# Joining loads in pairs and groups, and quantising two pieces at a time, in a fused two-layer Mamba, BitNet, attention and expert kernel

## The chip, the cores and the metric

The kernel runs on one core of a Trainium2 chip. The metric is device time in microseconds (us) of one launch. The core has five engines that work side by side, each through its own instructions in program order: TensorE (PE), VectorE (DVE), ScalarE (ACT), GpSimd (POOL) and SyncE (SP). In this kernel SP does nothing but issue DMAs, all of them, so every load, store and DMA transpose stands in one queue, and one that waits for its source or for a free buffer holds back all behind it.

## The reference

The input `x` has 4 batches of 512 rows of 512 features; `ctx` has 4 batches of 512 rows of 256. Two layers follow each other, each a mixer and a feed-forward part, both added to `x` through a tanh gate:

```
x = x + tanh(g_xattn[0]) * mamba(ctx_1024, layernorm(x))
x = x + tanh(g_ffn[0])   * bitnet_glu(layernorm(x))
x = x + tanh(g_xattn[1]) * cross_attention(layernorm(x), ctx_1024)
x = x + tanh(g_ffn[1])   * experts(layernorm(x))
```

- Mamba: 512 channels with 16 states each. For state n, step l: `state = state * exp(delta*A) + (delta*u) * B[n, l]` and `y += state * C[n, l]`. B and C are rows of 512 numbers, the same for all channels.
- BitNet GLU: three linear maps with activations rounded to 8-bit integers and ternary weights; `out(silu(gate(x)) * val(x))`, with 2048 inner values per row, gate and value biases, and a second rounding of the inner values with one scale per row.
- Cross attention: 16 heads of 128, queries and keys normalised, softmax over 512 keys, output projection `Wo`.
- Experts: four gated maps, each for a fixed quarter of the rows.

## The kernel before

Activations lie with 128 rows on the 128 partitions, so each batch is four blocks (`T = 4`). Products that need more than half precision use three matmuls on high and low f16 parts (`mm3`). A tile framework records the whole program, gives out buffers from tagged pools, and fixes the order of instructions on each engine with its own timing model; the recorded order sets the priorities. So a changed buffer or instruction also moves others.

**Stages, with their place in the profiled execution.** Weights are staged and the scan of batch 0 runs from about 55 to 180 us. The GLU of batch 0 and the staging of attention weights follow, to about 340 us. Then attention runs, 64 heads (4 batches, 16 heads), two heads ahead in the queries (a loop over `i`). Into the attention of batches 0, 1 and 2 the generator `layer0(b)` weaves scan and GLU of the next batch. Into the attention of batch 3 the experts of the first three batches are filled (`early_experts`); those of batch 3 end the kernel (`last_experts`).

**The scan (`scan`).** For batch 0 the four channel blocks are done together (`G = 4`), later two and two. For each state n the rows B[n] and C[n] are read from the DRAM scratch `bd`, each by its own DMA, and laid on all 128 partitions (`bc`, `cc`: lines 612 and 614). For each channel block ACT computes `dA = exp(delta*A)`, POOL computes `h = du * bc` (line 186, through `pool_mult`), DVE runs the recurrence (line 625, or 628 where POOL multiplies afterwards), and DVE (line 626) or POOL multiplies by `cc`. PE then transposes `h` and sums it in PSUM (line 593). `h` has six buffers under the tag `v`, shared with others.

**The GLU (`bitnet`).** `hidden(t)` makes the 2048 inner values of block t in four pieces `g` of 128x512. In batches 1 to 3 the tile of each piece is first filled with the gate bias by a DMA (line 709); DVE adds it to the scaled product (line 711). `project(t)` finds the row scale over all four pieces, and for each piece ACT scales and rounds (line 747) and DVE clamps to bf16 (line 748); pairs of pieces are transposed by DMA (line 750) and multiplied by the output weights. `hidden(t + 1)` is recorded before `project(t)`.

**The tag `g`.** `bc`, `cc`, the GLU's pieces and the experts' inner values (`it`, four for each expert, which all feed the down products `ped`) share six buffers of 2 KB a partition: `MIDS = {"g": 6, ...}`.

**Attention.** After each group of four heads `project(hg, os)` multiplies by the group's part of `Wo`: four loads of 256 KB into the tag `wo` with `WO = 4` buffers (line 977), and 4 x 12 matmuls `pwo`. For each half head SP also issues a transpose of the weights (`pT`, line 950), and for each block of keys two of `kT` (line 847). A softmax uses exp; the Ln of delta, the tanh of the GLU and the Silu of the experts need other ACT tables, so where these alternate in ACT's order, the compiler puts table loads.

Of the kernel before, what the change touches and what calls it, by code (L numbers as in the profile page):

```python
# [29 lines left out]
F32 = mybir.dt.float32  # L30
F16 = mybir.dt.float16
# [3 lines left out]
AF = mybir.ActivationFunctionType  # L35
# [5 lines left out]
P = 128  # L41
B = 4
L = 512
# [20 lines left out]
DVE_OF_8 = (0, 1, 2, 4, 5, 6)  # L64


MIDS = {"g": 6, "v": 6, "t": 4, "q": 2, "n": 1, "x": 1, "y": 2}
FILL0 = 4
RATE_S = 0.5
RATE_B = 0.8  # L70
# [40 lines left out]
def flamingo_kernel(  # L111
# [460 lines left out]
    def scan(b, of_8=DVE_OF_8, G=2, y_tile=lambda name: psum(pss, name), between=lambda n, ins: None):  # L572
        delta, du, ud_d, bd = fronts[b]
        sz_d = dram.tile([P, T, L], F32, tag="szd", name=f"szd{b}", bufs=2)

        def silu_z(t):

            xt = x_sb[b]
            w = normed(xt[:, t, :], row_stats(xt[:, t, :], f"z{b}{t}", 0.5), f"z{b}{t}")
            th = midt([P, L], F32, f"zth{b}{t}", "t")  # L580
            nc.scalar.activation(th, w, AF.Tanh)
            nc.vector.scalar_tensor_tensor(w, th, 1.0, w, ALU.add, ALU.mult)
            return w

        for t0 in range(0, T, G):
            gs = T // G
            ys = [y_tile(f"py{b}{t0}{i}").rearrange("p (g t e) -> p g t e", g=gs, t=G) for i in range(G)]

            def add(src, t, first, last):
                for g in range(T):
                    nc.tensor.matmul(  # L593
                        ys[g // gs][:, g % gs, t, :], src[:, g::T], ident, is_transpose=True,
                        start=first and t == 0 and g % gs == 0, stop=last, skip_group_check=True,
                    )

            uds, szs = [], []
            for t in range(G):
                uds.append(midt([P, L], F32, f"udr{b}{t0}{t}", "t"))  # L600
                nc.sync.dma_start(uds[t], ud_d[:, t0 + t, :])
            for n in range(DS):
                if n == 4 and x_sb[b] is None:
                    while b >= 2 and estats[b - 2] is None:
                        yield
                    load_x(b)
                if n == SZR and t0 > 0:
                    for t in range(t0, t0 + G):
                        szs.append(midt([P, L], F32, f"szr{b}{t}", "v"))
                        nc.sync.dma_start(szs[-1], sz_d[:, t, :])  # L610
                bc = midt([P, L], F32, f"bc{b}{t0}_{n}", "g")
                nc.sync.dma_start(bc, bd[n, :].partition_broadcast(P))
                cc = midt([P, L], F32, f"cc{b}{t0}_{n}", "g")
                nc.sync.dma_start(cc, bd[DS + n, :].partition_broadcast(P))
                for t in range(G):
                    nm = f"{b}{t0}{t}_{n}"
                    dA = psum(pss, f"dA{nm}")
                    last = nc.scalar.activation(  # L618
                        dA, delta[t0 + t], AF.Exp, scale=A[:, t0 + t, n : n + 1]
                    )  # L620
                    h = midt([P, L], F32, f"h{nm}", "v")
                    pool_mult(h, du[t0 + t], bc)

                    if (G * n + t) % 8 in of_8:
                        nc.vector.tensor_tensor_scan(dA, dA, h, 0.0, ALU.mult, ALU.add)  # L625
                        nc.vector.tensor_tensor(h, dA, cc, ALU.mult)  # L626
                    else:
                        nc.vector.tensor_tensor_scan(h, dA, h, 0.0, ALU.mult, ALU.add)
                        pool_mult(h, h, cc)
                    add(h, t, n == 0, n == DS - 1)  # L630
                    if n == 2:
                        add(uds[t], t, False, False)
                between(n, last.ins)
                yield

            xt = x_sb[b]
            if t0 == 0:
                szs = [silu_z(t) for t in range(T)]
                for t in range(G, T):
                    nc.sync.dma_start(sz_d[:, t, :], szs[t])  # L640
            for g in range(T):
                if g % gs == 0:
                    acc = midt([P, gs, G, P], F32, f"acc{b}{t0}{g}", "t")
                    nc.scalar.copy(acc, ys[g // gs])
                ps = transposed(pss, szs[:G], f"psz{b}{t0}{g}", g)
                a = acc[:, g % gs]
                nc.vector.tensor_tensor(a, a, ps, ALU.mult)
                xv = xt[:, g, :].rearrange("q (p e) -> q p e", e=T)[:, :, t0 : t0 + G]
                nc.vector.scalar_tensor_tensor(
                    xv, a.rearrange("q e p -> q p e"), tg[:, 0:1], xv, ALU.mult, ALU.add  # L650
                )
                yield
# [20 lines left out]
    def bitnet(b, w_tile=bigt, ps_tile=lambda name: psum(pss, name), biases=None, then=lambda t: None, g_tile=lambda name: psum(pss, name)):  # L673
# [23 lines left out]
        def hidden(t, xqT, sgv):  # L697

            nm = f"{b}{t}"
            hs = []  # L700
            mx = sm(4, "hmx", f"hmx{nm}")
            for n in range(4):
                cols = slice(n * 512, (n + 1) * 512)
                pg = g_tile(f"pg{nm}{n}")
                for k in range(T):
                    nc.tensor.matmul(pg, xqT[:, k, :], wg[:, k, cols], start=k == 0, stop=k == T - 1)
                g = midt([P, 512], F32, f"g{nm}{n}", "g")
                if biases is None:
                    nc.sync.dma_start(g, gate_b[cols].partition_broadcast(P))
                gb = g if biases is None else biases[0][:, cols]  # L710
                nc.vector.scalar_tensor_tensor(g, pg, sgv[:, 0:1], gb, ALU.mult, ALU.add)

                th = pg
                nc.scalar.activation(th, g, AF.Tanh, scale=0.5)
                pv = ps_tile(f"pv{nm}{n}")
                for k in range(T):
                    nc.tensor.matmul(pv, xqT[:, k, :], wv[:, k, cols], start=k == 0, stop=k == T - 1)
                v = midt([P, 512], F32, f"gv{nm}{n}", "v")
                if biases is None:
                    nc.sync.dma_start(v, val_b[cols].partition_broadcast(P))  # L720
                vb = v if biases is None else biases[1][:, cols]
                if (b, n) in GVP:
                    v2 = midt([P, 512], F32, f"gv2{nm}{n}", "t")
                    nc.scalar.activation(v2, pv, AF.Copy, scale=sgv[:, 1:2])
                    nc.gpsimd.tensor_tensor(v, v2, vb, ALU.add)
                else:
                    nc.vector.scalar_tensor_tensor(v, pv, sgv[:, 1:2], vb, ALU.mult, ALU.add)  # L727
                pool_mult(g, g, v)
                nc.vector.scalar_tensor_tensor(g, th, 1.0, g, ALU.add, ALU.mult)
                nc.vector.tensor_reduce(mx[:, n : n + 1], g, AX.X, ALU.max, apply_absolute_value=True)  # L730
                hs.append(g)
                yield

            return hs, mx

        def project(t, hs, mx):
# [2 lines left out]
            po = ps_tile(f"po{nm}")  # L739
            for i in range(2):  # L740
                hq = midt([P, 2, 512], BF16, f"hq{nm}{i}", "q" if b else "t")
                for j in range(2):
                    h = hs[2 * i + j]
                    if (b, 2 * i + j) in HQD:
                        nc.vector.tensor_scalar(h, h, up2, MAGIC, ALU.mult, ALU.add)
                    else:
                        nc.scalar.activation(h, h, AF.Identity, bias=magic, scale=up2)
                    nc.vector.tensor_scalar(hq[:, j], h, MAGIC, 127.0, ALU.subtract, ALU.min)
                hqT = midt([P, 8, P], BF16, f"hqT{nm}{i}", "q")
                nc.sync.dma_start_transpose(hqT, hq.rearrange("p j c -> p (j c)"))  # L750
                for k in range(8):
                    nc.tensor.matmul(po, hqT[:, k, :], wo[:, 8 * i + k, :], start=i + k == 0, stop=i == 1 and k == 7)
                yield
# [28 lines left out]
    def attention(b):  # L782
# [186 lines left out]
        def project(hg, os):  # L969
# [1 line left out]
            fo = sm(1, "fo", f"fo{nm}")  # L971
            nc.vector.tensor_scalar(fo, Sc[b][:, 0:1], Sv[hg][:, 0:1], 1.0 / QS, ALU.mult, ALU.mult)
            nc.vector.tensor_scalar(fo, fo, So[hg][:, 0:1], tg[:, 1:2], ALU.mult, ALU.mult)
            wos = []
            for h in range(HG):
                wo = at.tile([P, 2, 512], F16, tag="wo", name=f"wo{nm}{h}", bufs=WO)
                nc.sync.dma_start(wo.rearrange("p s c -> p (s c)"), wo_d[hg][:, h * 1024 : (h + 1) * 1024])
                wos.append(wo)
            for t in (T - 1, *range(T - 1)):
                rows = slice(t * P, (t + 1) * P)  # L980
                ps = ap(f"pwo{nm}{t}")
# [391 lines left out]
```

## Time and profile before

| | |
|---|---|
| time, median of 3 runs (lowest to highest) | 2031.38 us (2028.97 to 2038.59) |
| the profiled execution's own time | 2046.98 us |
| its span, first to last instruction | 2044.4 us |
| mean granted TensorE clock | 0.867 |
| busy: PE, DVE, ACT, POOL | 1613.0, 1576.5, 1321.8, 1000.7 us |
| DMA queue | 367.37 MB, 70.8% of 16 engines' span |
| issues on SP: `bc`, `cc` | 112 and 112, 256 KB each |
| issues on SP: gate bias `g`, `wo` | 48 and 64, 256 KB each |

The profile page gives, for one execution, the busy time of each engine, the same in 40 slices, and groups of equal instructions with their busy time, mean duration in ns, and the idle time of their engine just before them with what ended it. Other views of the same trace list instructions in order of time, waits by who waited for whom, the issues of SP with the time to landing, and busy time in chosen stretches. The profiled execution took 15.6 us longer than the median of the runs.

### The profile page before, as it was taken

How to read it: one execution, taken by the hardware profiler on the slowest of the kernel's cores; microseconds unless marked ns; L12 is line 12 of the kernel's file. 1: busy time of each engine (PE TensorE's matmuls, PEld its weight loads, DVE VectorE, ACT ScalarE, POOL GpSimd, SP SyncE). 2: the span in 40 equal slices, each digit the busy share in tenths (PEclk: the TensorE clock that was granted, in tenths of full speed). 3: DMA queues.
4: the chain of work that ended last, by engine and by line, in shares of the span. 5: the costliest groups of instructions: out<-in, count | busy, mean ns of one | idle time of the engine just before them, and what ended most of it. 6: DMA issues, size and time to landing. Idle time of an engine off the chain costs nothing. (4 is left out here: it accounts for less than half of the span.)

```text
span 2044.4 us, 27093 instructions
## 1 busy us (share of the span) xinstructions
PE 1613.0 (79%) x8238; PEld 903.5 (44%) x8238; DVE 1576.5 (77%) x2857; ACT 1321.8 (65%) x3118; POOL 1000.7 (49%) x926
## 2 busy tenths in 40 slices
PE   4465867666899877778988878778898879788888
PEld 1343322444544344454444444454444445445456
DVE  5898885999989788998987876999874455554554
ACT  5796566764758595665568663756477485757663
POOL 1884342875746378574436582765354240313211
PEclk8555987767889988898998988999999889898889
DMA  7554567788797877776658777787765686866754
GB/s 271 176 184 163 154 168 228 186 230 254 187 274 163 211 183 173 207 173 178 122 147 211 183 166 189 160 202 182 167 129 117 141 200 166 201 165 150 186 131 142
DMA packets 528242, 369.09 MB, mean 181 GB/s; under 512 B 425248, under 2 KB 427424, under 8 KB 521696
## 3 DMA queue, kind: packets, MB, share of 16 engines
q1 hardware_dynamic: 528096, 367.37, 70.8%
q8 instruction: 64, 1.05, 0.2%
q14 instruction: 82, 0.67, 0.1%
HBM read 220.22 MB, written 44.30 MB: 129 GB/s over the span
## 5 line engine op out<-in xcount | busy, mean ns | idle before, releaser
L186 POOL TENSOR_TENSOR h<-u,bc 128x512 f32<-128x512 f32 x256 | 337.6, 1339 | 83.9 <-PE py L593 49.1
L593 PE MATMUL py<-ident,h 128*128 128x128 f32 x1024 | 197.2, 337 | 134.3 <-DVE h L626 111.0
L618 ACT ACTIVATE dA<-delta,A 128x512 f32<-128x512 f32 x256 | 172.1, 685 | 136.0 <-DVE h L626 109.5
L625 DVE TENSOR_TENSOR_SCAN dA<-dA,h 128x512 f32<-128x512 f32 x200 | 240.7, 1217 | 20.3 <-POOL h L186 15.6
L252 PE MATMUL pav<-pT,v 128*128 128x256 f16 x1536 | 213.3, 294 | 49.2 <-DMA pT<-hl 36.2
L252 PE MATMUL ps<-kT,qT 128*128 128x512 f16 x768 | 215.9, 403 | 44.4 <-ACT pr L927 36.6
L252 PE MATMUL pq<-axnT,wq 128*128 128x512 f16 x768 | 211.6, 432 | 40.8 <-DMA axnT<-xsa 11.6
L593 PEld LDWEIGHTS py<-ident,h 128*128 128x128 f32 x1024 | 162.9, 212 | 179.2 <-DVE h L626 134.5
L948 DVE SCALAR_TENSOR_TENSOR hl<-pr,den,hl 128x512 f16<-128x512 f32 x214 | 195.2, 931 | 32.3 <-ACT hl L945 16.2
L907 DVE TENSOR_REDUCE nmx<-ps 128x1 f32<-128x512 f32 x256 | 172.6, 679 | 58.1 <-PE ps L252 57.5
L927 ACT ACTIVATE pr<-ps,nmx,rqs 128x512 f32<-128x512 f32 x256 | 197.6, 774 | 19.2 <-DVE hl L948 15.0
L252 PEld LDWEIGHTS <-v 128*128 128x128 f16 x1536 | 160.8, 106 | 110.1 <-issue 46.4
L252 PE MATMUL pwo<-wo,oT 128*128 128x512 f16 x768 | 184.7, 391 | 6.6 <-DVE oT L244 2.8
L947 POOL TENSOR_SCALAR hl<-pr,den 128x512 f16<-128x512 f32 x86 | 60.9, 708 | 213.8 <-issue 110.0
L252 PEld LDWEIGHTS <-wq 128*128 128x128 f16 x768 | 83.9, 110 | 153.8 <-issue 73.5
L252 PEld LDWEIGHTS <-cT 128*128 128x128 f16 x768 | 81.4, 107 | 137.5 <-issue 67.7
L186 POOL TENSOR_TENSOR g<-g,gv 128x512 f32<-128x512 f32 x64 | 83.7, 1309 | 110.3 <-DVE gv L727 55.5
L252 PEld LDWEIGHTS <-qT 128*128 128x128 f16 x768 | 78.5, 103 | 131.6 <-issue 64.4
L183 POOL TENSOR_TENSOR rqs<-ssq,mhalf 128x4 f32<-128x4 f32 x64 | 69.6, 1088 | 136.7 <-ACT ssq L896 133.7
L626 DVE TENSOR_TENSOR h<-dA,cc 128x512 f32<-128x512 f32 x200 | 133.5, 677 | 2.6
L252 PE MATMUL pk<-wk,cT 128*128 128x512 f16 x384 | 111.3, 437 | 23.8 <-DMA wk<-dwk 15.2
L945 ACT ACTIVATE hl<-pr,den 128x512 f16<-128x512 f32 x128 | 92.1, 719 | 56.1 <-DVE den L934 48.6
(373 smaller groups left out, 3512.6 us busy)
## 6 DMA issues: line engine op xcount, KB each, us to landing
bc<-bd SPq DMA_DIRECT2D x112, 256.0 KB, 4.3
cc<-bd SPq DMA_DIRECT2D x112, 256.0 KB, 4.2
wq<-dwq SPq DMA_DIRECT2D x64, 256.0 KB, 4.1
wo<-dwo SPq DMA_DIRECT2D x64, 256.0 KB, 4.4
w<-w3d SPq DMA_DIRECT2D x12, 1024.0 KB, 7.7
g<-in_gate_b SPq DMA_DIRECT2D x48, 256.0 KB, 4.3
gv<-in_val_b SPq DMA_DIRECT2D x48, 256.0 KB, 4.2
de<-hle SPq DMA_DIRECT2D x9, 1024.0 KB, 5.8
```

The lines of the kernel that those rows point to most:

```text
L183: nc.gpsimd.tensor_tensor(res, arg, mhalf[:, : arg.shape[1]], ALU.pow)
L186: nc.gpsimd.tensor_tensor(out, a, b, ALU.mult)
L252: nc.tensor.matmul(ps, l, r, start=first and i == 0, stop=last and i == n - 1)
L593: nc.tensor.matmul(ys[g // gs][:, g % gs, t, :], src[:, g::T], ident, is_transpose=True, start=first and t == 0 and g % gs == 0, stop=last ...
L618: last = nc.scalar.activation(dA, delta[t0 + t], AF.Exp, scale=A[:, t0 + t, n : n + 1])
L625: nc.vector.tensor_tensor_scan(dA, dA, h, 0.0, ALU.mult, ALU.add)
L626: nc.vector.tensor_tensor(h, dA, cc, ALU.mult)
L907: nc.vector.tensor_reduce(nmx[:, c : c + 1], ps, AX.X, ALU.max, negate=True)
L927: mark[0] = nc.scalar.activation(pr, scs[c], AF.Exp, bias=nmx[:, one], scale=rqs[:, one], accum_out=den[:, c - c0 : c - c0 + 1],).ins
L945: nc.scalar.activation(hl[:, c, 0], prs[c], AF.Copy, scale=den[:, one])
L947: nc.gpsimd.tensor_scalar(hl[:, c, 0], prs[c], den[:, one], 1.0, ALU.mult, ALU.mult)
L948: nc.vector.scalar_tensor_tensor(hl[:, c, 1], prs[c], den[:, one], hl[:, c, 0], ALU.mult, ALU.subtract)
```

## The change

Four edits. (1) B[n] and C[n] of a state come by one DMA of 512 KB into one tile `bcc` of two rows, and `bc`, `cc` are its halves; the tag `g` has three buffers of 4 KB in place of six of 2 KB. (2) The GLU's pieces lie in pairs in one tile `g2`; in batches 1 to 3 one DMA brings the gate bias of a pair. (3) A pair is rounded by one ACT and clamped by one DVE instruction of 128x1024. (4) A head group's output weights come by one DMA of 1 MB into one buffer `wo`. The experts' `it` tiles are as they were, but now share three buffers.

```diff
-MIDS = {"g": 6, "v": 6, "t": 4, "q": 2, "n": 1, "x": 1, "y": 2}
+MIDS = {"g": 3, "v": 6, "t": 4, "q": 2, "n": 1, "x": 1, "y": 2}
...
-                bc = midt([P, L], F32, f"bc{b}{t0}_{n}", "g")
-                nc.sync.dma_start(bc, bd[n, :].partition_broadcast(P))
-                cc = midt([P, L], F32, f"cc{b}{t0}_{n}", "g")
-                nc.sync.dma_start(cc, bd[DS + n, :].partition_broadcast(P))
+                bcc = midt([P, 2, L], F32, f"bcc{b}{t0}_{n}", "g")
+                nc.sync.dma_start(bcc, bd.rearrange("(s n) l -> n s l", s=2)[n].partition_broadcast(P))
+                bc, cc = bcc[:, 0], bcc[:, 1]
...
-                g = midt([P, 512], F32, f"g{nm}{n}", "g")
-                if biases is None:
-                    nc.sync.dma_start(g, gate_b[cols].partition_broadcast(P))
+                if n % 2 == 0:
+                    g2 = midt([P, 2, 512], F32, f"g{nm}{n}", "g")
+                    if biases is None:
+                        nc.sync.dma_start(
+                            g2.rearrange("p a c -> p (a c)"),
+                            gate_b[n * 512 : (n + 2) * 512].partition_broadcast(P),
+                        )
+                    hs.append(g2)
+                g = g2[:, n % 2]
...
-                for j in range(2):
-                    h = hs[2 * i + j]
-                    if (b, 2 * i + j) in HQD:
-                        nc.vector.tensor_scalar(h, h, up2, MAGIC, ALU.mult, ALU.add)
-                    else:
-                        nc.scalar.activation(h, h, AF.Identity, bias=magic, scale=up2)
-                    nc.vector.tensor_scalar(hq[:, j], h, MAGIC, 127.0, ALU.subtract, ALU.min)
+                nc.scalar.activation(hs[i], hs[i], AF.Identity, bias=magic, scale=up2)
+                nc.vector.tensor_scalar(hq, hs[i], MAGIC, 127.0, ALU.subtract, ALU.min)
...
-            wos = []
-            for h in range(HG):
-                wo = at.tile([P, 2, 512], F16, tag="wo", name=f"wo{nm}{h}", bufs=WO)
-                nc.sync.dma_start(wo.rearrange("p s c -> p (s c)"), wo_d[hg][:, h * 1024 : (h + 1) * 1024])
-                wos.append(wo)
+            wo = at.tile([P, HG, 2, 512], F16, tag="wo", name=f"wo{nm}", bufs=1)
+            nc.sync.dma_start(wo.rearrange("p h s c -> p (h s c)"), wo_d[hg])
+            wos = [wo[:, h] for h in range(HG)]
```

More of the change, by code (lines that the diff above doesn't have):

```diff
@@ L730, in hidden @@
                 nc.vector.tensor_reduce(mx[:, n : n + 1], g, AX.X, ALU.max, apply_absolute_value=True)
-                hs.append(g)
                 yield
```

## The prediction

> **What bounds the kernel now.** I read the page first: no engine fills the span, DVE works hardest until about 1500 us (slice 29), PE after it.
>
> ```profile
> PE   4465867666899877778988878778898879788888
> DVE  5898885999989788998987876999874455554554
> DMA  7554567788797877776658777787765686866754
> ```
>
> Then the busy time of the three stretches in which a scan is woven into attention (batches 1, 2, 3): DVE is busy for 665.82 of 752 us, 89%, so what stalls DVE there moves the end.
>
> ```profile
> sum 752.00, PE 577.15 PEld 350.55 DVE 665.82 ACT 492.80 POOL 507.12; mean PE 192.38 PEld 116.85 DVE 221.94 ACT 164.26 POOL 169.04
> ```
>
> Next the groups: how often the scan waits. POOL's product sat idle for 83.9 us, 22.6 of them for B's load; DVE's recurrence waited 15.6 us for POOL.
>
> ```profile
> L186 POOL TENSOR_TENSOR h<-u,bc 128x512 f32<-128x512 f32 x256 | 337.6, 1339 | 83.9 <-PE py L593 49.1 <-DMA bc<-bd 22.6 <-DVE nmx L907 4.4
> L625 DVE TENSOR_TENSOR_SCAN dA<-dA,h 128x512 f32<-128x512 f32 x200 | 240.7, 1217 | 20.3 <-POOL h L186 15.6 <-ACT dA L618 4.4
> ```
>
> Last, SP's own waits (total us, times, longest): the load of C waits for DVE's multiply (line 626), the load of B mostly for POOL's product (line 186), which is done long before. Beside them the SP time of one issue (min/median/max, ns), and the landing times by size.
>
> ```profile
> SPq L614 <- DVE h L626: 84.2, 26, 5.9
> SPq L612 <- POOL h L186: 54.8, 38, 5.1
> L612 SPq DMA_DIRECT2D bc<-bd x112: 319/382/1587, 42.7 to 1358.2; - x112
> bc<-bd SPq DMA_DIRECT2D x112, 256.0 KB, 4.3
> wv<-dwv SPq DMA_DIRECT2D x12, 512.0 KB, 5.0
> wk<-dwk SPq DMA_DIRECT2D x16, 512.0 KB, 5.6
> rawe<-in_gate_up SPq DMA_DIRECT2D x16, 512.0 KB, 6.8
> ```
>
> **Edit 1, B and C in one load.** It removes 112 issues, 112 x 0.38 = 43 us of SP. What it moves matters more. Three states are in flight before and after, but B's buffer used to come free after the second product of a state; now it comes free with C's, after the last multiply, and B[n+3] can only be asked for then. So POOL's first product of n+3 lies behind: issue 0.38, landing 5.6 (`wk`, the middle one of the 512 KB rows), product 1.27 (POOL's median); 7.25 us from the last use of state n to the recurrence of n+3. What the order of before leaves for it I took from the timelines of POOL and DVE, state by state: for the 78 states of batches 1 to 3 that reuse a buffer, the time from the last multiply by C[n] to the first recurrence of n+3 has a median of 9.9 us. Under 6.6 (the landing of `wv`) are 3 of 78, short by 4.4 us together; under 7.25, 4, by 6.6 us; under 8.0, 10, by 11.5 us; under 9.0 (the landing of `rawe`, and 1.8 for a product, the longest in the trace), 21, by 27.8 us. I take 8.0, 0.75 over the bare sum, because SP issues transposes that hold it: the 128 `pT` take 2.87 us each, 367 us in all, by the SP timeline. DVE waits in order, so a shortfall stalls the attention work queued behind that recurrence too: **+11.5 us**, ends +4.4 and +27.8. Below nothing it would go only through SP, counted below. In batch 0 the same interval is 10.8 us at least, so 2.8 us of DVE's work on the other channel blocks still cover the load: 0; were it gone, 13 states would lose what exceeds 10.8.
>
> One stall of before shows the mechanism. POOL stood 2.48 us for a B that SP had issued late:
>
> ```profile
> 484.27 4.63 POOL L186 TENSOR_TENSOR h<-u,bc 128x512 f32<-128x512 f32 x3
> 491.38 1.27 POOL L186 TENSOR_TENSOR h<-u,bc 128x512 f32<-128x512 f32 x1 [2.48 <-DMA bc<-bd]
> ```
>
> By the fit in "SBUF — State Buffer" of the Trainium skill, section "The DMA setup-cost knee", about 2 us plus bytes at 436 GB/s, doubling 256 KB would add only 0.6 us, an estimate; the need would be 6.55 us and this term about 4 in place of 11.5, but the landing rows of this trace rise by 0.7 to 2.5 us. A rule of "DMA: Bandwidth & Descriptors", section "Rules for kernel authors", speaks against the edit: issue the DMA early and wait for it late; B's load is issued later, and by that rule the upper end, +27.8, is the one to take.
>
> **Edit 2, gate bias by pairs.** 48 loads become 24, 9 us of SP. DVE waited for gate biases 7.7 us, in 4 waits. A pair is freed when both halves are clamped and lands 5.6 - 4.3 = 1.3 us later; with 0.4 for the second clamp 1.7 us for each of 4 waits, 7 at most. In the changed kernel's order the pieces that reuse a buffer stand behind up to 1 us more DVE work: **+2**, ends 0 and +7. Batch 0 takes its biases from a resident tile: 0.
>
> **Edit 3, rounding in pairs.** The rows are
>
> ```profile
> L747 ACT ACTIVATE g<-g,magic,quph 128x512 f32<-128x512 f32 x64 | 47.0, 803 | 18.3 <-DVE quph L668 18.3
> L748 DVE TENSOR_SCALAR hq<-g 128x512 bf16<-128x512 f32 x64 | 37.4, 616 | 13.5 <-DMA hqT<-hq 10.8 <-ACT g L747 2.6
> L243 ACT ACTIVATE wv<-rawv,Swv 128x1024 f16<-128x1024 f32 x4 | 4.6, 1138 | 0.7 <-DVE Swv L221 0.7
> L565 ACT ACT_TABLE_LOAD x11 | 14.1, 1283 | 0.2
> ```
>
> ACT: 32 x 1.14 = 36.4 for 47.0, 10.6 us less, but ACT is busy 65% of the span and DVE is late next, so 0 of it counts. DVE: two chained clamps took 0.75 us, two single ones 0.41 each, so joining saves 0.07 x 32: **-2**. Nothing reaches the transpose earlier, since it needed both halves before.
>
> **Edit 4, `Wo` in one load.** 64 loads become 16, 48 x 0.38 = 18 us of SP. 1 MB rows land in 5.0 to 8.5 us, four loads in 4.4 + 3 x 0.38 = 5.5. The cover: the last four loads of before were issued by 1929.0 and first used about 1990, 60 us later: 0. Uncovered, 16 x 2.2 = 35 us.
>
> **What the order shows besides.** ACT has 42 table loads for 38: 4 x 1.28 = 5.1 us. Around the fronts of the scans as many are lost as gained; the four lie in the last batch's attention, where exp and the experts' Silu alternate more often, and there PE waits for ACT's exp (10.5 us after 1500 us), though ACT is busy for only some 33 of each 50 us: half of it, **+2.6**, ends 0 and +5.1. The experts' fourth `it` now waits for the down products of the first, three buffers for four tiles; PE's order there is nearly the same and ends identically from the last head on, so I take 0, at most 4 x 0.83 (twelve matmuls of the final chain) = 3.3.
>
> **SP.** It issues 184 DMAs fewer, 70 us of the roughly 1000 it spends issuing. POOL, PE and DVE stood for DMAs 120 us in all (`pT` 36.2, `bc` 22.6, `wk` 15.2, `hqT` 18.6, `axnT` 11.6, `g` 7.7, smaller ones 8); 70/1000 of that is 8, and half of it ends in another wait: **-4**, ends 0 and -20 (the fall of issues, 17%, in place of the time's 7%).
>
> The sum is 11.5 + 2 - 2 + 2.6 - 4 = **+10 us**: the profiled execution would go from 2046.98 to 2057, and the median, 15.6 us below it, from 2031.4 to **2041**. No change in bytes moved, so the DMA share of 0.76 to 0.82 in the scans stays as it is.
>
> **The rivals.** *POOL starves attention* (slower by much). POOL's first product began a median 4.5 us after the last use of C[n], but 6.0 is the least now (0.38 + 5.6); 52 of 78 began earlier, 198 us of lateness together. POOL is in order, and behind a product that waits stand `rqs`, `rk` and the f16 casts of the softmax; others waited for these and for `h` 76.5 us (ACT 25.0 for `rqs`, DVE 21.7 for `rk`, 14.2 for casts, 15.6 for `h`). If that grows by half, +38: 2069. It decides once lateness exceeds POOL's own slack; against it, POOL is idle 33% in these stretches and its order was made anew. *SP relief wins* (faster): if the 120 us fall by 17%, -20, with -2 of DVE and +4 of the sum's other terms, -18: 2013. For it: SP is the only issuer. Against: its longest holds, the `pT` issues, stay. *All is hidden*: the new order spreads each recurrence far enough, 0 +- 5: 2031. That the change does not do what it says is excluded: SP's order has 112, 24 and 16 loads.
>
> **How the numbers follow.** 0.5%, about what a measurement of this kernel can tell from no change, is 10.2 us: 2021.2 to 2041.5. The forecast, +2 to +18, has 0.50, and lies half on each side of that bound: 0.25 and 0.25. POOL starving, +20 to +45, 0.17, slower. Relief, -11 to -26, 0.22, faster. All hidden, 0.11, same. Faster 0.22, same 0.36, slower 0.42. The range reaches -19 into relief and +35 into starving: 2012 to 2066.
>
> **What would show it.** Right: `h` waits for `bcc` for longer than 22.6 us and the recurrence for POOL longer than 15.6; landing near 5.6; 42 table loads; SP's wait before `bcc` names line 626 or POOL's multiply; the first 180 us and the last 60 keep their length. Wrong: `h` waits less for its load, or landing under 5 us (relief, or hidden), or the difference lies in a stretch without a scan, after 1400 us, which my sum gives only 2.6.

## The result and the profile after

The changed kernel takes 2048.76 us, median of 7 runs (2046.26 to 2056.25), against 2036.33 us of the kernel before (7 runs, 2028.97 to 2038.59). The medians lie 12.4 us apart; the ratio estimated over all these runs is 1.0076, with a 95% interval of 1.0057 to 1.0096: slower by 15.5 us (11.6 to 19.5).

The two profiled executions hide this. Their spans are 2044.4 us before and 2044.3 after, since the one of before took 10.7 us more than its median and the one of after 2.5 less. So the two traces can't be subtracted as wholes; stages and waits must be compared.

The page of the kernel after, busy tenths of PE and DVE in 40 slices: DVE, the fullest engine until slice 29, has 7 nines for 11 in slices 7 to 29 (counted from 0); slices 25 to 27, the last scan, went from 9 9 9 to 7 8 8.

```profile
PE   4464866657789975978898787788899888898888
DVE  5898885889989777889997885788985465555654
```

The windows view from 1500 us to the end (busy us and instruction counts of PE, PEld, DVE, ACT, POOL, then granted TensorE clock, DMA share, GB/s), first of before, then of after:

```profile
1500.00:2044.00 544.00, 470.01 (x2734) 263.00 (x2732) 294.61 (x591) 344.40 (x908) 148.31 (x156) 0.92 0.66 159
```

```profile
1500.00:2044.00 544.00, 478.27 (x2873) 271.56 (x2870) 318.32 (x637) 363.50 (x951) 160.84 (x169) 0.96 0.68 166
```

After has 139 PE and 46 DVE instructions more behind 1500 us: work that was pushed back by then. It is done in the same 544 us, at a granted clock of 0.96 against 0.92. The lateness is visible ahead of this: the last scan's last multiply is at 1379.7 us before and at 1409.7 after, 30 us later. Measured scan by scan, from the first recurrence to the last multiply, the six scans woven into attention take 552.8 us before and 594.0 after; the scan of batch 0 takes 120.6 and 122.6.

The groups of the kernel after (busy us, mean ns | idle time ahead of them, and what ended it). POOL's product stood for its load 86.3 us where it had stood 22.6, DVE's recurrence for POOL 37.3 where it had been 15.6:

```profile
L186 POOL TENSOR_TENSOR h<-u,bcc 128x512 f32<-128x512 f32 x256 | 333.8, 1324 | 129.3 <-DMA bcc<-bd 86.3 <-PE py L593 27.1 <-DVE acc L646 5.7
L624 DVE TENSOR_TENSOR_SCAN dA<-dA,h 128x512 f32<-128x512 f32 x200 | 241.3, 1218 | 49.7 <-POOL h L186 37.3 <-ACT dA L617 9.1 <-ACT ksq L824 2.8
```

SP's waits and issues after (total us, times, longest; min/median/max ns of an issue; KB and us to landing, counted from the start of the issue). The joint load now waits for the last use of a state: 109.3 us for DVE's multiply by C, and of the 72.0 us for POOL 69.9 for POOL's multiply by C (2.1 for its first product). The clamp of the GLU's pieces (`hq`), which share the tag, holds it for 9.6 us; before it held the loads of B and C for 13.4. 512 KB land in 6.1 us:

```profile
SPq L612 <- DVE h L625: 109.3, 37, 8.1
SPq L612 <- POOL h L186: 72.0, 34, 9.5
L612 SPq DMA_DIRECT2D bcc<-bd x112: 359/371/1312, 43.2 to 1389.9; - x112
bcc<-bd SPq DMA_DIRECT2D x112, 512.0 KB, 6.1
g<-in_gate_b SPq DMA_DIRECT2D x24, 512.0 KB, 4.7
```

One stall, from the timelines of POOL, SP and DVE after (start, duration, engine, instruction [idle before it <- what ended it]). It is state 8 of a half scan, which takes the buffer of state 5. The last multiply by C of state 5, on POOL, is over at 412.34; SP issues the load from 412.36 (the second of the row is the next state's, issued at 412.83); POOL, with nothing else to do from 414.65 on, stands until the load is there, and starts the product at 418.63; it takes some 1.25 us; DVE, in order, stands 3.38 us until 419.93, with the attention work queued behind. From the last use to the recurrence these are 7.6 us:

```profile
410.62 1.72 POOL L186 TENSOR_TENSOR h<-h,bcc 128x512 f32<-128x512 f32 x1
```

```profile
412.36 0.88 SPq L612 DMA_DIRECT2D bcc<-bd  x2
```

```profile
418.63 2.48 POOL L186 TENSOR_TENSOR h<-u,bcc 128x512 f32<-128x512 f32 x2 [3.98 <-DMA bcc<-bd]
```

```profile
419.93 1.23 DVE L624 TENSOR_TENSOR_SCAN dA<-dA,h 128x512 f32<-128x512 f32 x1 [3.38 <-POOL h L186]
```

The waits by engine after (total us, times, longest) show whether attention suffered with the scan. Waits for `h` grew on DVE (15.6 before) and on PE (15.8 before); those for `rk` (21.7), `rqs` (25.0) and the casts (14.2) did not grow together:

```profile
DVE dA L624 <- POOL h L186: 37.3, 17, 7.1
DVE ksq L835 <- POOL rk L183: 29.5, 20, 4.0
DVE hl L947 <- POOL hl L946: 11.2, 16, 1.2
ACT nmx L918 <- POOL rqs L183: 20.8, 20, 2.0
PE py L593 <- POOL h L186: 34.5, 16, 9.1
```

### The profile page after: what moved, and what is told of

The parts are those of the page before. It is cut to its first block, busy times and chain, and to the rows that moved or that the text cites. A ratio compares the mean times of both kernels' runs of the same rounds, so it can differ in the third digit from the quotient of the medians.

```text
span 2044.3 us, 26624 instructions
## 1 busy us (share of the span) xinstructions
PE 1595.1 (78%) x8238; PEld 899.7 (44%) x8238; DVE 1564.7 (77%) x2825; ACT 1322.4 (65%) x3090; POOL 1002.6 (49%) x926
## 5 line engine op out<-in xcount | busy, mean ns | idle before, releaser
L186 POOL TENSOR_TENSOR h<-u,bcc 128x512 f32<-128x512 f32 x256 | 333.8, 1324 | 129.3 <-DMA bcc<-bd 86.3
L593 PE MATMUL py<-ident,h 128*128 128x128 f32 x1024 | 203.0, 345 | 148.5 <-DVE h L625 102.9
L624 DVE TENSOR_TENSOR_SCAN dA<-dA,h 128x512 f32<-128x512 f32 x200 | 241.3, 1218 | 49.7 <-POOL h L186 37.3
L252 PE MATMUL pav<-pT,v 128*128 128x256 f16 x1536 | 209.0, 291 | 60.3 <-DMA pT<-hl 32.3
L252 PE MATMUL pq<-axnT,wq 128*128 128x512 f16 x768 | 201.2, 416 | 25.1 <-DVE ksq L835 6.5
L947 DVE SCALAR_TENSOR_TENSOR hl<-pr,den,hl 128x512 f16<-128x512 f32 x214 | 188.4, 895 | 24.0 <-ACT hl L944 12.4
L946 POOL TENSOR_SCALAR hl<-pr,den 128x512 f16<-128x512 f32 x86 | 65.2, 758 | 193.1 <-DVE den L933 93.0
L625 DVE TENSOR_TENSOR h<-dA,bcc 128x512 f32<-128x512 f32 x200 | 133.9, 678 | 2.9
L252 PEld LDWEIGHTS <-oT 128*128 128x128 f16 x768 | 76.8, 102 | 107.9 <-issue 22.5
```

The lines of the kernel that those rows point to most:

```text
L186: nc.gpsimd.tensor_tensor(out, a, b, ALU.mult)
L252: nc.tensor.matmul(ps, l, r, start=first and i == 0, stop=last and i == n - 1)
L593: nc.tensor.matmul(ys[g // gs][:, g % gs, t, :], src[:, g::T], ident, is_transpose=True, start=first and t == 0 and g % gs == 0, stop=last ...
L946: nc.gpsimd.tensor_scalar(hl[:, c, 0], prs[c], den[:, one], 1.0, ALU.mult, ALU.mult)
L947: nc.vector.scalar_tensor_tensor(hl[:, c, 1], prs[c], den[:, one], hl[:, c, 0], ALU.mult, ALU.subtract)
```

## The experiments

The theory: joining B with C lets B's buffer go only after the last multiply by C, so B[n+3] is asked for too late, whether it comes by one load or two. The rivals: the joint load lands later (6.1 us for 4.3); one of the other edits costs it, the pairing of the GLU's pieces among them, which no run has without that of B and C; the experts' `it` tiles, four of which now share three buffers; and the new order of instructions as such, which any edit brings. Each kernel was timed against the kernel before in five rounds, and the ratios are to it.

**Paired buffers alone.** The kernel before, with pairs of 4 KB for B and C and for the GLU's pieces; every load, rounding step and `Wo` stays separate.

```diff
-MIDS = {"g": 6, ...
+MIDS = {"g": 3, ...
...
-                bc = midt([P, L], F32, f"bc{b}{t0}_{n}", "g")
+                bcc = midt([P, 2, L], F32, f"bcc{b}{t0}_{n}", "g")
+                bc, cc = bcc[:, 0], bcc[:, 1]
                 nc.sync.dma_start(bc, bd[n, :].partition_broadcast(P))
-                cc = midt([P, L], F32, f"cc{b}{t0}_{n}", "g")
                 nc.sync.dma_start(cc, bd[DS + n, :].partition_broadcast(P))
...
-                g = midt([P, 512], F32, f"g{nm}{n}", "g")
+                if n % 2 == 0:
+                    g2 = midt([P, 2, 512], F32, f"g{nm}{n}", "g")
+                    hs.append(g2)
+                g = g2[:, n % 2]
...
```

> Only the buffers are paired (three of 4 KB); every load, rounding step and the four loads of Wo stand as before. Late release theory: B's buffer is freed only with C's, so most of the loss is here already: ratio to before 1.005 to 1.009, POOL's products wait for B's load 50 to 80 us (22.6 before, 86.3 changed), the recurrence for POOL over 28 us. Late landing theory (one 512 KB load lands 1.8 us later than a 256 KB one): ratio within 1.000 to 1.003, waits for B near 30 us. Theory that three buffers for four expert tiles and the four more table loads make the loss: 1.003 to 1.006, with the waits of the scan near before's.

Measured: 1.0100 (1.0060 to 1.0141). Groups and landing of this kernel:

```profile
L186 POOL TENSOR_TENSOR h<-u,bcc 128x512 f32<-128x512 f32 x256 | 334.4, 1327 | 119.8 <-DMA bcc<-bd 65.7
L625 DVE TENSOR_TENSOR_SCAN dA<-dA,h 128x512 f32<-128x512 f32 x200 | 241.4, 1218 | 39.0 <-POOL h L186 29.9
```

With no load joined and no issue saved, POOL's wait is three times that of before and the time is at least that of the whole change. For the waits the pairing of the buffers is enough; that it is enough for the time too rests on one comparison of 1%, and the runs below show that one such comparison can't carry it alone. (The profiled execution is the slowest of the six, 14 us over their median.)

**B and C by two loads into the pair.** The kernel after, with one line changed.

```diff
-                nc.sync.dma_start(bcc, bd.rearrange("(s n) l -> n s l", s=2)[n].partition_broadcast(P))
+                nc.sync.dma_start(bc, bd[n, :].partition_broadcast(P))
+                nc.sync.dma_start(cc, bd[DS + n, :].partition_broadcast(P))
```

> The changed kernel, but B and C come by two loads of 256 KB into the halves of the joint tile. Late release theory: stays slow, 1.005 to 1.009, POOL waits for B 60 to 85 us, scans of batch 3 end 20 us or more later than before's. Late landing theory: the loss goes, 0.999 to 1.003, POOL waits for B under 40 us.

Measured: 1.0018 (0.9993 to 1.0044). The landing falls to 4.9 us, POOL's wait to 54.1 and the recurrence's to 18.9 us. Against the kernel after (1.0076) this is 0.6% better. The theory of the late release missed here: the ratio is in the range of the late landing, POOL's wait in neither range, and the last scan ends 6.5 us earlier than in the kernel before (1373.2 us for 1379.7), not 20 later. So the longer landing of one load looked like a second cause; the later runs qualify this.

**`Wo` alone.** The kernel before with edit 4.

```diff
-            wos = []
-            for h in range(HG):
-                wo = at.tile([P, 2, 512], F16, tag="wo", name=f"wo{nm}{h}", bufs=WO)
-                nc.sync.dma_start(wo.rearrange("p s c -> p (s c)"), wo_d[hg][:, h * 1024 : (h + 1) * 1024])
-                wos.append(wo)
+            wo = at.tile([P, HG, 2, 512], F16, tag="wo", name=f"wo{nm}", bufs=1)
+            nc.sync.dma_start(wo.rearrange("p h s c -> p (h s c)"), wo_d[hg])
+            wos = [wo[:, h] for h in range(HG)]
```

> The kernel before with Wo of a head group in one 1 MB load and one buffer, nothing else. Late release and late landing theories: 0.998 to 1.002, no wait of pwo for its load. If the Wo load took part in the loss: 1.003 or more, with pwo matmuls waiting for wo.

Measured: 1.0013 (0.9990 to 1.0035). 48 issues fewer bring nothing that shows, and no `pwo` waits for its weights: no worth of edit 4 shows either way.

**Two of the experts' tiles in one buffer.** The kernel after; the four `it` tiles of an expert take two of the three buffers, so the fourth doesn't wait for the down products of the first.

```diff
-            it = it_tile([P, 2, n], F16, f"it{nm}{i}")
+            if i % 2 == 0:
+                it2 = it_tile([P, 2, 2, n], F16, f"it{nm}{i}")
+            it = it2[:, i % 2]
```

> The changed kernel, but the experts' four it tiles lie two by two in a buffer, so all four of an expert fit in two of the three. Late release and late landing theories: 1.006 to 1.009 as changed. Theory that the experts' three buffers made the loss: 1.000 to 1.004, and the stretch after 1500 us 5 us or more shorter.

Measured: 1.0147 (1.0113 to 1.0182), above both ranges and slower still than the kernel after, with nearly the same waits in the scan (82.1 and 40.3 us). So nothing speaks for the experts' three buffers as the cost. Why the relaxed version is 0.7% slower was not found; its last scan ends at 1411.2 us, 1.5 after that of the kernel after, so nearly all of the difference lies behind the scans.

**A fourth pair, and its control.** A fourth pair needs 4 KB a partition. They come from `pT`, the transposed softmax weights, which get two buffers for three; the control changes only that.

```diff
-PT = 3
+PT = 2
```

> The changed kernel with two buffers for pT in place of three, as a control for the next run, which needs their 4 KB. All theories: as the changed kernel or a little slower, ratio to before 1.005 to 1.02; POOL waits for bcc 70 to 100 us, the recurrence for POOL over 28 us.

Measured: 1.0049 (1.0029 to 1.0068), just under the 1.005 that was expected at least, with the waits as expected.

```profile
L186 POOL TENSOR_TENSOR h<-u,bcc 128x512 f32<-128x512 f32 x256 | 331.6, 1315 | 117.9 <-DMA bcc<-bd 71.1
L624 DVE TENSOR_TENSOR_SCAN dA<-dA,h 128x512 f32<-128x512 f32 x200 | 241.4, 1220 | 34.7 <-POOL h L186 28.0 <-ACT dA L617 6.1
```

```diff
-MIDS = {"g": 3, "v": 6, ...
+MIDS = {"g": 4, "v": 6, ...
...
-PT = 3
+PT = 2
```

> The same with a fourth joint buffer of 4 KB, so the load of state n+3 needs the buffer of n-1 and not of n: the landing stays 512 KB, the late release no longer matters. Late release theory: POOL waits for bcc fall under 35 us, the six half scans together (594.0 us changed, 552.8 before) fall under 565, and the ratio to before falls at least 0.006 below that of the two-buffer control. Late landing theory, by which the size of the load and not its start makes the loss: waits stay above 60 us, and the ratio falls by under 0.003.

Measured: 0.9904 (0.9880 to 0.9929), with the joint load and all else of the change in place:

```profile
L186 POOL TENSOR_TENSOR h<-u,bcc 128x512 f32<-128x512 f32 x256 | 333.1, 1320 | 92.6 <-PE py L593 42.8 <-DMA bcc<-bd 30.7 <-DVE h L625 8.1
L624 DVE TENSOR_TENSOR_SCAN dA<-dA,h 128x512 f32<-128x512 f32 x200 | 241.1, 1219 | 25.7 <-POOL h L186 14.8 <-ACT dA L617 10.5
```

The only difference in the source from the control is the fourth pair. (The GLU's pieces and the experts' tiles share it, and the order is new.) POOL's wait for the load falls from 71.1 to 30.7 us, the recurrence's from 28.0 to 14.8 (before had 15.6), the six scans from 572.5 to 532.1 us, and the time by 1.45%. The landing is the same 6.1 us as in the kernel after. All three things expected of the late release came true. This is the strongest single result for the theory: give the joint buffer its time back by one more, and the cost is gone.

**Joint rounding, and one gate load, each added to the paired buffers.** The base is the first experiment (1.0100).

```diff
-                for j in range(2):
-                    h = hs[i][:, j]
-                    nc.scalar.activation(h, h, AF.Identity, bias=magic, scale=up2)
-                    nc.vector.tensor_scalar(hq[:, j], h, MAGIC, 127.0, ALU.subtract, ALU.min)
+                nc.scalar.activation(hs[i], hs[i], AF.Identity, bias=magic, scale=up2)
+                nc.vector.tensor_scalar(hq, hs[i], MAGIC, 127.0, ALU.subtract, ALU.min)
```

> Paired buffers with all loads separate (1.0100), plus the joint rounding alone. It asks which edit made the changed kernel with split B and C loads (1.0018) faster than paired buffers alone. If the rounding gives it: 1.000 to 1.004, scans of batch 3 end 20 us or more earlier than 1412. If it is the relief of SP by fewer loads, or the order that the scheduler happens to choose: 1.007 to 1.013.

Measured: 1.0052 (1.0033 to 1.0070), 0.5% better than its base and between the two ranges. The last scan ends at 1390.3 us, 21.7 earlier than in the base (1412.0), as was expected if the rounding gives it.

```diff
+                    if biases is None:
+                        nc.sync.dma_start(
+                            g2.rearrange("p a c -> p (a c)"),
+                            gate_b[n * 512 : (n + 2) * 512].partition_broadcast(P),
+                        )
...
-                if biases is None:
-                    nc.sync.dma_start(g, gate_b[cols].partition_broadcast(P))
```

> Paired buffers with all loads separate (1.0100), plus the gate bias by one load for a pair. If fewer issues on SP give the gain: 1.002 to 1.006 (24 of the 72 issues that the three other edits save). If the rounding gives it: 1.008 to 1.012.

Measured: 1.0094 (1.0074 to 1.0115), as its base: 24 issues fewer bring nothing that shows.

**The other way round: joint rounding undone.** The kernel after with the four lines of rounding taken apart again (the inverse of the first of the two diffs above).

```diff
-                nc.scalar.activation(hs[i], hs[i], AF.Identity, bias=magic, scale=up2)
-                nc.vector.tensor_scalar(hq, hs[i], MAGIC, 127.0, ALU.subtract, ALU.min)
+                for j in range(2):
+                    h = hs[i][:, j]
+                    nc.scalar.activation(h, h, AF.Identity, bias=magic, scale=up2)
+                    nc.vector.tensor_scalar(hq[:, j], h, MAGIC, 127.0, ALU.subtract, ALU.min)
```

> The changed kernel with ACT and DVE rounding each piece by itself (edit 3 undone). The profiles showed the clamp at 37.4 us for 64 single and 25.4 us for 32 joint ones. If that saving counts in full on DVE's path: ratio to before 1.011 to 1.015. If it is as small as the -2 us of the prediction: 1.006 to 1.009.

Measured: 1.0040 (1.0021 to 1.0060). This missed both ranges: without joint rounding the kernel after is 0.4% faster, while adding it to the paired buffers had made those 0.5% faster. The two signs can't both be the worth of the edit. What is common to both is that the order of all engines was made anew.

**Four pairs with two loads.** The fourth pair, and B and C by their own loads.

```diff
-MIDS = {"g": 3, "v": 6, ...
+MIDS = {"g": 4, "v": 6, ...
...
-PT = 3
+PT = 2
...
-                nc.sync.dma_start(bcc, bd.rearrange("(s n) l -> n s l", s=2)[n].partition_broadcast(P))
+                nc.sync.dma_start(bc, bd[n, :].partition_broadcast(P))
+                nc.sync.dma_start(cc, bd[DS + n, :].partition_broadcast(P))
```

> The four-pair kernel (0.9904) with B and C by two loads. Late release theory: with four pairs in flight the landing of 512 KB is hidden, so the split gains nothing: 0.988 to 0.994. Late landing theory: the split gains again as it did with three (1.0018 for 1.0076): 0.982 to 0.987.

Measured: 0.9862 (0.9834 to 0.9890), 2003.07 us: the fastest version of all, faster than both kernels. The ratio is in the range of the late landing.

```profile
L186 POOL TENSOR_TENSOR h<-u,bcc 128x512 f32<-128x512 f32 x256 | 337.2, 1336 | 79.4 <-PE py L593 35.9 <-DMA bcc<-bd 28.9 <-DMA cS<-cTd 4.1
L625 DVE TENSOR_TENSOR_SCAN dA<-dA,h 128x512 f32<-128x512 f32 x200 | 240.4, 1216 | 19.1 <-POOL h L186 9.9 <-ACT dA L618 8.6
```

It lies 0.4% under the joint load with four pairs, but the intervals overlap.

**The kernel before with the control's constant, and with eight single buffers.** The first has one line changed.

```diff
-PT = 3
+PT = 2
```

> The kernel before with two pT buffers, the control for the eight-buffer run. All theories: 0.998 to 1.004, as the changed kernel with two pT buffers was no slower than with three.

Measured: 0.9891 (0.9863 to 0.9920). This too missed: taking one buffer from `pT` makes the kernel before 1.1% faster, with waits in the scan only a little shorter (15.6 us for `bc`, 12.3 for `h`). Why was not found. It changes what the last runs say: with two `pT` buffers three pairs cost 1.6% (1.0049 against 0.9891), and four pairs (0.9904, 0.9862) are about as fast as the kernel before, not clearly faster. So the speed of the fastest version goes with the `pT` constant; the four edits show no gain in it.

The second has two more single buffers as well, the bytes of four pairs.

```diff
-MIDS = {"g": 6, "v": 6, ...
+MIDS = {"g": 8, "v": 6, ...
...
-PT = 3
+PT = 2
```

> The kernel before with two pT buffers and eight 2 KB buffers in place of six for B, C and the GLU's pieces: as deep as four pairs, with B still released early and every load separate. If depth alone made the four-pair kernel 0.9904: 0.985 to 0.993. If the four-pair kernel gains from the edits once the late release is paid for: 0.995 to 1.002 here.

Measured: 0.9959 (0.9937 to 0.9981). With eight single buffers POOL no longer waits for `bc` at all,

```profile
L186 POOL TENSOR_TENSOR h<-u,bc 128x512 f32<-128x512 f32 x256 | 336.0, 1337 | 68.2 <-PE py L593 55.8 <-PE psz L485 10.4 <-DVE oT L244 0.6
```

and the kernel is 0.7% slower than with six. The range that was named for a gain of the edits in the four-pair kernel is met, but against its own control (0.9891) that kernel has no gain. The recurrence waits for POOL as long as with six (13.3 us for 12.3), so the last 15 us of POOL's wait for `bc` were not on its way.

**All kernels together.** A single comparison of 1% or less can't be trusted here (one `pT` buffer moved the kernel before by 1.1%), but the groups part, if narrowly:

| kernels | POOL waits for B, us | recurrence waits for `h`, us | ratio |
|---|---|---|---|
| three pairs, PT 3: after and six experiments | 54 to 94 | 18.9 to 40.3 | 1.0018 to 1.0147, mean 1.0075 |
| three pairs, PT 2 (control) | 71.1 | 28.0 | 1.0049 |
| six singles, PT 3: before, `Wo` alone | 22.6, 18.0 | 15.6, 11.7 | 1, 1.0013 |
| four pairs, six singles, eight singles, PT 2: four experiments | 0 to 30.7 | 9.9 to 14.8 | 0.9862 to 0.9959, mean 0.9904 |

By its point value every kernel with three pairs is slower than every one of the six without, if only just at the ends (1.0018 and 1.0013): by 0.7% on the means at PT 3, by 1.45% at PT 2. The end of the last scan parts them on the means too, 1399.9 us against 1375.0 at PT 3, 1379.9 against 1359.4 at PT 2, so the loss is there by the time the scans end. Within the first group the waits don't order the times: the recurrence waits 19.1 us in the kernel at 1.0094 and 37.2 in the one at 1.0040.

Of the eight kernels with three pairs, the four with one joint load (after, the experts' tiles, the control, rounding undone) have a mean of 1.0078, and the four with separate loads (paired buffers, the two additions to them, two loads in after) 1.0066. So the joint load as such costs 0.1%, of the size of nothing, by the groups, and 0.4 to 0.6% by the two direct pairs. A third pair has the other sign: rounding undone (1.0040) differs from paired buffers with one gate load (1.0094) by the joint load and the joint `Wo`, and is 0.5% faster. A cost of the late landing isn't shown; this stays open.

## Why the prediction was right, and where its sizes were off

The sign, the mechanism and the place were right: the measured +15.5 us lies within the forecast's own +2 to +18, above its middle of +10. That the sum came so near is in part luck: its largest term was 10 us too small, another 10 us too small the other way. And the forecast time of 2041 us stood on a base of 2031.4; the seven runs put that at 2036.33. By its steps:

- **Edit 1, right in kind, too small.** The term of the sum that was mis-sized is the +11.5 us for 10 of 78 states. Measured: the recurrence waited 37.3 us in 17 places for 15.6 in 8, +21.7, between the 11.5 and the upper end of 27.8. The bare chain has a slip: landing is counted from the start of the issue, so the 0.38 stands in the 7.25 us twice, and 5.6 + 1.27 = 6.9 was meant; now it is 6.1 + 1.32 = 7.4, and 7.6 in the stall shown above. The 8.0 that was taken covers both. What failed was to take the intervals of the order of before as the budget, with few states short. In the new order POOL's first product of n+3 begins a median 8.3 us after the last use of C[n] (4.5 before), the recurrence 11.9 us after it (9.9 before): the median state is later, not a tail of ten. That the late release makes the waits is shown by the paired buffers alone (22.6 to 65.7 us) and by the fourth pair (71.1 to 30.7). That it makes the time rests on the fourth pair (1.0049 to 0.9904) and on the groups of the table; next to it a share of the longer landing isn't excluded.
- **The page against the row.** The fit of the Trainium skill's "SBUF — State Buffer", section "The DMA setup-cost knee", would have doubled the load for 0.6 us; this trace has 4.3 us for 256 KB and 6.1 for 512 KB, 1.8 more, so the rows were the better source. The rule of "DMA: Bandwidth & Descriptors", section "Rules for kernel authors", to issue early and wait late, gives a direction and no size; that was right here. The prediction put its upper end, +27.8, beside it, and the +21.7 measured lies nearer to that than to the 11.5 that I took.
- **Edit 2, nothing.** Gate biases are waited for 6.2 us in 4 waits, 7.7 before, not +2: a pair lands in 4.7 us, not the 5.6 assumed. One gate load for a pair, added to the paired buffers, made no difference (1.0094 against 1.0100).
- **Edit 3, DVE's part mis-sized.** ACT fell from 47.0 to 37.9 us, 9.1 less, near the 10.6 predicted. The clamps fell from 37.4 to 25.4 us, 12.0 less, where -2 was in the sum; over all kernels single clamps take 29.6 to 38.9 us (mean 34.2 of seven) and joint ones 23.5 to 29.2 (mean 25.8 of seven), so about 8 us of DVE. The medians are steady, 417 to 421 ns for a single clamp in its seven kernels and 685 to 693 for a joint one in its seven, so joining saves 32 x (2 x 0.420 - 0.686) = 4.9 us by these, not 2; the rest is that fewer clamps are long, 6 of 32 for 17 of 64. It is busy time on the fullest engine, and would set against part of edit 1; but the two runs that isolate it disagree in sign (-0.5%, +0.4%), so its worth in time was not settled.

```profile
L746 ACT ACTIVATE g<-g,magic,quph 128x1024 f32<-128x1024 f32 x32 | 37.9, 1231 | 8.3 <-DVE quph L667 8.3
L747 DVE TENSOR_SCALAR hq<-g 128x1024 bf16<-128x1024 f32 x32 | 25.4, 799 | 17.9 <-DMA hqT<-hq 7.4 <-ACT ssq L895 5.8 <-ACT g L746 4.7
```

The joint clamps after, by the view of their tile (min/median/max ns; the single ones before have 405, 420 and 1546):

```profile
L747 DVE TENSOR_SCALAR hq<-g x32: 675/686/1754, 236.4 to 1544.5; 128x1024 bf16<-128x1024 f32 x32
```

- **Edit 4, nothing that shows, as predicted** (1.0013). The experts' buffers at 0 stand too, as far as the one run on them goes.
- **SP relief, not shown.** SP has 184 issues fewer (1082 to 898), and its issuing time went from 997 to 939 us, 58 and not 70; with the same 1082 issues two other kernels took 966 and 1020. The 120 us that POOL, PE and DVE stood for DMAs were read too small: the "smaller ones" are 44 us and not 8, 156 in all. Without B's and C's loads these waits went from 132.7 to 118.7 us, while ACT's went from 23.6 to 41.7; with ACT the sum hardly moves (156.3 to 160.4). The runs with 48 and 24 issues fewer (1.0013, and 1.0094 against 1.0100) show no gain, so no run shows the -4, and the rival that rests on it (2013 us, faster) is out. Of SP's waits, 181 us ahead of the joint load were for buffers of the scan.
- **Table loads**, 42 for 38, came as the order showed. But the wait from which the +2.6 was argued, PE's for ACT's exp after 1500 us, fell from 10.5 to 6.5 us, so its row speaks against the term. Over the other kernels the loads run from 36 to 42 without a pattern in the time.
- **The rival of starved attention** had the right row and the wrong neighbours: its four waits went from 76.5 to 98.8 us, +22, but all of that is `h` itself (+21.7); `rqs`, `rk` and the casts went from 60.9 to 61.5.

The terms as measured add up to about 21.7 - 1.5 - 12.0 = +8 on DVE; the +15.5 holds some 7 us that no row of the profiled pair explains. PE's wait for `h` grew by 18.7 us and may hold part of it; with new orders moving the time by as much, I can't show it.

What the prediction left out altogether is that last point: the range was made of mechanisms alone, while an edit that touches none of them (one buffer of `pT`, and the order that follows from it) moved the kernel before by -1.1% and the kernel after by -0.3%.

## What to carry to other kernels

When two operands are put into one tile, the one that was free early is held until the other is: look for what asks for its next contents, and pay with one more buffer, or keep separate tiles. Don't count a saved DMA issue as time while the issuing queue waits for buffers: here 48 and 24 fewer showed nothing. Where a scheduler makes the order anew at every edit, run a few edits that should change nothing before crediting or blaming one of 1% or less, compare with a control that has the same constants, and trust what holds over a group of orders.

## What the runs showed of the hardware

A broadcast load to 128 partitions landed in 4.3 us for 256 KB and in 6.1 us (4.7 to 10.5) for 512 KB; two of 256 KB issued one after the other in 4.7 to 5.2 each, in the four kernels with three pairs and separate loads.

The same clamp of 128x512 took from 488 to 639 ns in the mean from one order to another, and the joint one of 128x1024 from 743 to 918, with medians that hardly moved. The difference is a few long ones, up to 1.55 and 1.75 us. In the kernel before all 17 clamps that took over 0.5 us overlap in time with a POOL instruction that combines two tensors, and of the 38 that overlap with none the longest took 0.43; after, all 6 long ones overlap with one, too. Not every overlap makes one long (9 of 26 before don't), and no run changes it alone, so this is what goes together, not a tested cause.

Two executions with nearly equal spans had granted clocks of 0.92 and 0.96 over the last 544 us. If all of that stretch went with the clock, this would be some 23 us, an upper estimate; a difference of 0.76% is 15.5.
